# Second edge stage of a two-layer graph network: VectorE inputs from PSUM, a one-hot on ScalarE, macros of 16 groups, earlier row loads

## The chip, the cores and the metric

The kernel runs on one core of a Trainium2 chip, and the metric is the device time of that core in microseconds: the median of three runs of the whole program. A fourth execution was taken by the hardware profiler. All rows, durations and moments below are of that one.

## What is computed

Two graph layers over 6250 nodes with 128 features and 100000 edges, sorted by destination. The kernel's second edge stage, where most of the change lies, belongs to the second layer, an attention layer with four heads of 32 channels:

```python
src = jnp.concatenate([src, loop]); dst = jnp.concatenate([dst, loop])
xl = (x @ w_l + b_l).reshape(N, H, C)
xr = (x @ w_r + b_r).reshape(N, H, C)
e = jax.nn.leaky_relu(xl[src] + xr[dst], NEG_SLOPE)
logits = jnp.einsum('ehc,hc->eh', e, att)
m = jax.ops.segment_max(logits, dst, num_segments=N)
ex = jnp.exp(logits - m[dst])
denom = jax.ops.segment_sum(ex, dst, num_segments=N)
alpha = ex / denom[dst]
out = jax.ops.segment_sum(xl[src] * alpha[:, :, None], dst, num_segments=N)
```

The first layer gathers node rows by source, adds a projection of the edge features, applies relu and averages per destination. Both layers end in a residual add and a layer norm.

## The kernel before, in words

All edges lie in order of destination, 128 to a tile; four tiles (512 edges) are a group, and there are 196 groups. The destinations of one group lie within a window of 96 rows (`W`), so the sum over edges is a product with a one-hot matrix of 128 edges by 96 rows (`onehot`, L315). The window's first row comes from `first_row` (L322), which loads the group's first destination from DRAM into a register of SyncE.

The program has node stages and two edge stages. The **first edge stage** (L326 to L386) gathers one source row per edge through GpSimd (`gather`, L242, four indirect DMAs a group), adds the edge projection (L375, VectorE, PSUM input), applies relu (L377), sums with the one-hot (L380) and stores the window (L386).

The **second edge stage** (L399 to L564) goes over the groups in macros of 20 (nine of 20, then 12 and 4). For each group:

- `load_second` gathers 512 rows of `xl` (four indirect DMAs on GpSimd) and has SyncE load the window of `xr` (L424, needs `first_row`) and the destination numbers of the group, one copy in each of 96 partitions, `ds` (L426).
- `logits`: VectorE compares `ds` with the row numbers `nb` (L433) to get `at`, the transposed one-hot; TensorE transposes the four `xl` tiles into `pz` (L436) and adds `xr` times `at` (L438); ScalarE copies `pz` to `z` (L440), VectorE applies the leaky relu (L441), and TensorE multiplies by the attention weights into `plg` (L443), which collects a whole macro.
- `sums`, for the groups of the macro before: ScalarE and VectorE weight the gathered rows (`v`, L527 and L528), VectorE makes the one-hot (L315), TensorE sums (L533), VectorE scales what the group before left in its last row (`old`, L537), TensorE adds it (L539), ScalarE copies the window out of PSUM (`win`, L542), and SyncE stores it (L543, needs `first_row` again).

After a macro's last group `maxima` (L448 to L519) loads the destinations once more (`dm`, L454, four DMAs on SyncE) and works out the segment maxima and weights of all its groups in a chain of small steps over VectorE, ScalarE and TensorE. The sums of a macro can start only when its `maxima` is done, and are spread over the logits of the next one.

The order on SyncE is the order in which the code is written (`tc.manual_schedule(engines={SP})`): in each step the rows of group g+3, then the stores. On the other engines a scheduler lays out a fixed order when the program is built, by its own estimate of when each input is there; at run time each engine works through that order and stands still when the next instruction's input is late. The buffers are those named with `bufs`: 28 for the gathered rows, 5 for `xr` and `ds`, 3 for `at`, 4 for `win`, two PSUM banks each for `pz` and `pa`.

Of the kernel before, what the change touches and what calls it, by code (L numbers as in the profile page):

```python
# [8 lines left out]
F32 = mybir.dt.float32  # L9
# [6 lines left out]
P = 128  # L16
# [23 lines left out]
S = G * P  # L40
TV = -(-E // P)
NOWHERE = 1e6
MACROS = (20,) * 9 + (12, 4)
MG = max(MACROS)
HV = C + 2
CR, CC = 125, 800
# [13 lines left out]
def gnn_resnorm(  # L60
# [87 lines left out]
    def over(t, n):  # L148

        return t.unsqueeze(1).to_broadcast([t.shape[0], n, t.shape[1]])  # L150
# [96 lines left out]
    def near():  # L247
        ctx = ExitStack()
        with ctx:
# [11 lines left out]
                           allow_small_or_imprecise_dtypes=True)  # L261
            nc.gpsimd.iota(iota_p, pattern=[[0, 1]], base=0, channel_multiplier=1,
                           allow_small_or_imprecise_dtypes=True)

            with tc.tile_pool(name="ix", bufs=2) as pool, tc.tile_pool(name="ixp", bufs=2, space=PSUM) as ps:
                zero = pool.tile([P, NR // P * H * HV], F32, name="zero", bufs=1)
                nc.gpsimd.memset(zero, 0.0)
                for t, n in ((sum_t, W0), (out_t, H * HV)):
                    nc.scalar.dma_start(t.rearrange("(p r) d -> p (r d)", p=P), zero[:, 0:NR // P * n])
                nc.scalar.dma_start(xr_t[NP:NR, :], zero[:, 0:D])  # L270

                fst = pool.tile([1, GN], I32, name="fst", bufs=1)
                nc.sync.dma_start(fst, bass.AP(tensor=dst.tensor, offset=dst.offset, ap=[[S, 1], [S, GN], [1, 1]]))
                fst_f = pool.tile([1, GN], F32, name="fst_f", bufs=1)
                nc.vector.tensor_copy(fst_f, fst)
                pb = ps.tile([P, GN], F32, name="pb", bufs=1)
                nc.tensor.matmul(pb, ones[0:1, :], fst_f, start=True, stop=True)
                bb = pool.tile([P, GN], F32, name="bb", bufs=1)
                nc.vector.tensor_copy(bb, pb)
                nc.vector.tensor_scalar(nb, bb, iota_p, None, op0=OP.add)  # L280
                step = pool.tile([P, GN], F32, name="step", bufs=1)
                nc.vector.memset(step, 0.0)
                nc.vector.tensor_sub(step[:, 1:], bb[:, 1:], bb[:, 0:GN - 1])
                nc.vector.tensor_scalar(sel, step, iota_p, None, op0=OP.is_equal)


                TR = 112
                for name, ap, pad in (("src", src, 0), ("dst", dst, int(NOWHERE))):
                    rows = pool.tile([TR, T // TR, P], I32, name="rows")
                    nc.vector.memset(rows[:, T // TR - 1, :], pad)  # L290
                    full = E // P
                    o = T - TR
                    nc.sync.dma_start(rows[:, 0:T // TR - 1, :],
                                      ap[0:o * P].rearrange("(c r p) -> r c p", r=TR, p=P))
                    nc.sync.dma_start(rows[0:full - o, T // TR - 1, :],
                                      ap[o * P:full * P].rearrange("(r p) -> r p", p=P))
                    nc.sync.dma_start(rows[full - o:full - o + 1, T // TR - 1, 0:E - full * P],
                                      ap[full * P:E].rearrange("(r p) -> r p", r=1))
                    rf = pool.tile([TR, T // TR, P], F32, name="rf")
                    nc.vector.tensor_copy(rf, rows)  # L300
                    for c in range(T // TR):
                        pt = ps.tile([P, TR], F32, name="pt")
                        nc.tensor.transpose(pt, rf[:, c, :], ident[0:TR, 0:TR])
                        cs = slice(c * TR, (c + 1) * TR)
                        if name == "src":
                            nc.vector.tensor_copy(src_i[:, cs], pt)
                        else:
                            nc.vector.tensor_sub(dl[:, cs].rearrange("p (g k) -> p g k", k=G),
                                                 pt.rearrange("p (g k) -> p g k", k=G),
                                                 spread(bb[:, c * TR // G:(c + 1) * TR // G], G))  # L310

            def onehot(pool, g):

                a = pool.tile([P, G, W], F32, name="a")
                nc.vector.tensor_tensor(a, over(iota_w, G), spread(dl[:, g * G:(g + 1) * G], W), op=OP.is_equal)  # L315
                return a

            def tiles_of(g):
# [80 lines left out]
            with tc.tile_pool(name="e1", bufs=3) as pool, tc.tile_pool(name="e1m", bufs=2) as mp, \  # L399
# [14 lines left out]
                        nc.vector.tensor_copy(attw[mg][hs, (h + 1) * mg:(h + 1) * mg + 1], att_c[hs])  # L414
                XG, XR, DS = {}, {}, {}

                def load_second(g):
                    XG[g] = pool.tile([P, G, D], F32, name="xg", bufs=MG + 8)
                    if len(tiles_of(g)) < G:
                        nc.vector.memset(XG[g], 0.0)  # L420
                    for t in tiles_of(g):
                        gather(XG[g][:, t - g * G, :], xl_t, src_i, t)
                    XR[g] = pool.tile([W, D], F32, name="xr", bufs=5)
                    nc.sync.dma_start(XR[g], xr_t[bass.ds(first_row(g), W), :])  # L424
                    DS[g] = pool.tile([W, S], F32, name="ds", bufs=5)
                    nc.sync.dma_start(DS[g], bass.AP(tensor=dpad.tensor, offset=dpad.offset + 1 + g * S,  # L426
                                                     ap=[[0, W], [1, S]]))

                def logits(m, g):

                    g0, mg, plg = m
                    at = pool.tile([W, S], F32, name="at")
                    nc.vector.tensor_scalar(at, DS.pop(g), nb[0:W, g:g + 1], None, op0=OP.is_equal)  # L433
                    pz = ps.tile([P, S], F32, name="pz")
                    for j in range(G):
                        nc.tensor.matmul(pz[:, j * P:(j + 1) * P], XG[g][:, j, :], ident, is_transpose=True,  # L436
                                         start=j == 0, stop=False, skip_group_check=True)
                    nc.tensor.matmul(pz, XR.pop(g), at, start=False, stop=True, skip_group_check=True)  # L438
                    z = pool.tile([P, S], F32, name="z")
                    nc.scalar.copy(z, pz)  # L440
                    nc.vector.scalar_tensor_tensor(z, z, SLOPE, z, op0=OP.mult, op1=OP.max)  # L441
                    i = g - g0
                    nc.tensor.matmul(plg, attw[mg][:, mg - i:mg - i + H * mg], z, start=i == 0, stop=i == mg - 1)  # L443

# [78 lines left out]
                def sums(m, g, wm, cb):  # L523
                    i = g - m[0]
                    xg = XG.pop(g)
                    v = pool.tile([P, G, H, HV], F32, name="v")
                    nc.scalar.copy(v[:, :, :, 0:2], wm[:, :, :, :, i].rearrange("p j k h -> p j h k"))  # L527
                    nc.vector.tensor_tensor(v[:, :, :, 2:], xg.rearrange("p j (h c) -> p j h c", h=H),  # L528
                                            wm[:, :, 0, :, i].unsqueeze(3).to_broadcast([P, G, H, C]), op=OP.mult)
                    a = onehot(pool, g)  # L530
                    pa = ps.tile([W, H * HV], F32, name="pa")
                    for j in range(G):
                        nc.tensor.matmul(pa, a[:, j, :], v[:, j].rearrange("p h c -> p (h c)"),  # L533
                                         start=j == 0, stop=j == G - 1)
                    if before[0] is not None:
                        old = pool.tile([W, H, HV], F32, name="old")
                        nc.vector.tensor_tensor(old, before[0].rearrange("p (h c) -> p h c", h=H),  # L537
                                                spread(cb[0:W, :, i], HV), op=OP.mult)
                        nc.tensor.matmul(pa[0:1, :], sel[0:W, g:g + 1], old.rearrange("p h c -> p (h c)"),  # L539
                                         start=False, stop=True, skip_group_check=True)  # L540
                    before[0] = pool.tile([W, H * HV], F32, name="win", bufs=4)
                    nc.scalar.copy(before[0], pa)  # L542
                    nc.sync.dma_start(out_t[bass.ds(first_row(g), W), :], before[0])  # L543

                ahead = 3
                for g in range(ahead):
                    load_second(g)
                done, g0 = None, 0
                for mg in MACROS:
                    plg = ps1.tile([H * mg, S], F32, name="plg")  # L550
# [3 lines left out]
                    for i in range(mg):  # L554
                        g = g0 + i
                        if g + ahead < GN:
                            load_second(g + ahead)
                        logits(m, g)
                        for u in todo[i * n // mg:(i + 1) * n // mg]:
                            sums(done[0], u, *done[1])  # L560
# [359 lines left out]
```

## Time and profile before

| | us |
|---|---|
| median of three runs (3266.94 to 3286.33) | 3269.77 |
| the profiled execution's own time | 2644.76 |
| its span, first to last instruction | 2643.0 |
| first edge stage, first to last gather issued | 98.1 to 1085.5 |
| second edge stage, first gather issued to last store issued | 1233.5 to 2517.5 |
| busy in the span: PE / DVE / ACT / POOL | 1664.0 / 1054.5 / 490.4 / 1623.6 |
| mean granted TensorE clock | 0.807 of full |

The profiled execution is shorter than the timed runs by 625 us. PE is TensorE, PEld its weight loads, DVE VectorE, ACT ScalarE, POOL GpSimd, and SPq the queue of SyncE. SyncE's register work and DMA issues are not counted as busy time in the page, so they have to be read from its queue in order of time. A row of a group of instructions gives line, engine, operation, output and inputs, how many, then busy us and mean ns of one, then the engine's idle time before them and what ended it. In waits the three numbers are us in total, times and the longest.

### The profile page before, as it was taken

Reading aid. Unit: us, or ns where it says so; the run is one execution under the profiler, and the core shown is the slowest. Engines: PE = TensorE matmul, PEld = TensorE weight load, DVE = VectorE, ACT = ScalarE, POOL = GpSimd, SP = SyncE. Lnnn points to the kernel's source line nnn. Section 1 sums busy time; section 2 is a strip of 40 time slices with the busy share of each in tenths; the row PEclk is TensorE's granted clock in tenths of the full one; section 3 lists DMA queues with packets and bytes.
Section 4 is the critical chain, followed back from the end, with each engine's and each line's share of the span. In section 5 each row is a group of like instructions: output and inputs, shape, how many; then the busy total and the mean of one; then the engine's idle time right before and its main releaser. Section 6 shows DMA issues by size and latency. Waiting matters only on the chain.

```text
span 2643.0 us, 29233 instructions
## 1 busy us (share of the span) xinstructions
PE 1664.0 (63%) x7133; PEld 1004.1 (38%) x7133; DVE 1054.5 (40%) x2386; ACT 490.4 (19%) x1369; POOL 1623.6 (61%) x1574
## 2 busy tenths in 40 slices
PE   5376666666666666444677767776767777677500
PEld 3254444444444444322233433343434344343300
DVE  4322222222222222375233534353535445354578
ACT  1122222222222212110111212121212112121101
POOL 0477777777777777302777776767676776763000
PEclk9678887888878877766788888888888889898655
DMA  4633334333433333222323333333333333332021
GB/s 117 184 88 84 85 87 93 87 87 86 95 86 86 87 93 84 70 67 84 102 73 98 93 100 88 100 85 102 84 99 85 94 96 86 101 85 66 17 57 49
DMA packets 289799, 232.01 MB, mean 88 GB/s; under 512 B 140697, under 2 KB 244487, under 8 KB 289362
## 3 DMA queue, kind: packets, MB, share of 16 engines
q1 hardware_dynamic: 231466, 116.99, 16.5%
q0 software_dynamic: 50048, 102.60, 16.1%
q10 hardware_dynamic: 8104, 10.46, 1.1%
q8 instruction: 60, 0.98, 0.2%
q14 instruction: 121, 0.99, 0.1%
HBM read 189.85 MB, written 40.03 MB: 87 GB/s over the span
## 4 chain that ended last, share of the span: by engine, by line
POOL 28%; issue 20%; DMA 16%; PE 14%; DVE 13%; SPq 7%; ACT 2%; DVEq 0%; ACTq 0%; POOLq 0%
POOL xg L242 28%; DMA ds<-dpad 7%; SPq L322 5%; DMA xg<-xw_t,src_i 4%; PE pa L533 3%; PE pz L438 3%; PE plg L443 2%; DMA xg<-xl_t,src_i 2%; DVE z L441 2%; PE pw L231 1%; DVE v L528 1%; PE pw L205 1%; PE pa L539 1%; DVE at L433 1%; DMA xr_t<-zero 1%
## 5 line engine op out<-in xcount | busy, mean ns | idle before, releaser
L242 POOL DMA_INDIRECT xg<-xl_t,src_i x782 | 867.3, 1109 | 454.2 <-issue 212.4
L242 POOL DMA_INDIRECT xg<-xw_t,src_i x782 | 749.5, 958 | 259.1 <-issue 224.9
L373 PE MATMUL ph<-wc,fT 128*128 128x256 f32 x784 | 289.9, 501 | 283.0 <-ACT fT L370 283.0
L443 PE MATMUL plg<-z,attw 128*80 128x512 f32 (+2 forms) x392 | 260.0, 752 | 175.3 <-DVE z L441 175.0
L375 DVE TENSOR_TENSOR xg<-ph,xg 128x512 f32<-128x512 f32 x196 | 135.6, 692 | 544.0 <-DMA xg<-xw_t,src_i 433.5
L433 DVE TENSOR_SCALAR at<-ds,nb 96x512 f32<-96x512 f32 x196 | 99.3, 507 | 573.6 <-DMA ds<-dpad 519.8
L438 PE MATMUL pz<-at,xr 96*128 96x512 f32 x392 | 254.4, 737 | 86.8 <-DVE at L433 86.7
L380 PE MATMUL pa<-msg,a 128*96 128x129 f32 x1568 | 269.5, 325 | 53.9 <-ACT msg L377 53.9
L373 PEld LDWEIGHTS ph<-wc,fT 128*128 128x128 f32 x784 | 177.0, 253 | 328.7 <-ACT fT L370 303.0
L315 DVE TENSOR_TENSOR a<-iota_w,dl 128x384 f32<-128x384 f32 x392 | 216.7, 554 | 208.4 <-PE pa L380 202.0
L533 PEld LDWEIGHTS pa<-v,a 128*96 128x96 f32 x1568 | 227.4, 184 | 117.8 <-issue 98.2
L533 PE MATMUL pa<-v,a 128*96 128x136 f32 x1568 | 258.0, 310 | 8.4 <-DVE v L528 6.3
L380 PEld LDWEIGHTS pa<-msg,a 128*96 128x96 f32 x1568 | 220.4, 194 | 108.5 <-ACT msg L377 60.9
L377 ACT ACTIVATE msg<-xg 128x512 f32<-128x512 f32 x196 | 123.5, 630 | 723.0 <-DVE xg L375 723.0
L440 ACT COPY z<-pz 128x512 f32<-128x512 f32 x196 | 114.9, 586 | 731.0 <-PE pz L438 712.9
L436 PE MATMUL pz<-ident,xg 128*128 128x128 f32 x784 | 168.4, 312 | 54.2 <-DMA xg<-xl_t,src_i 48.4
L436 PEld LDWEIGHTS pz<-ident,xg 128*128 128x128 f32 x784 | 106.0, 156 | 213.8 <-issue 125.1
L441 DVE SCALAR_TENSOR_TENSOR z<-z 128x512 f32<-128x512 f32 x196 | 133.8, 684 | 58.7 <-ACT z L440 56.5
L443 PEld LDWEIGHTS plg<-z,attw 128*80 128x80 f32 (+2 forms) x392 | 56.3, 173 | 240.5 <-DVE z L441 203.4
L528 DVE TENSOR_TENSOR v<-xg,wm 128x512 f32<-128x512 f32 x196 | 132.5, 685 | 31.9 <-issue 13.6
L438 PEld LDWEIGHTS pz<-at,xr 96*128 96x128 f32 x392 | 73.6, 232 | 116.9 <-DVE at L433 114.0
L382 PE MATMUL pa<-win,sel 96*1 96x129 f32 x390 | 86.6, 310 | 12.8 <-ACT win L385 12.4
(162 smaller groups left out, 1160.3 us busy)
## 6 DMA issues: line engine op xcount, KB each, us to landing
ds<-dpad SPq DMA_DIRECT2D x196, 192.0 KB
ef<-in_edge_attr_dram SPq DMA_DIRECT2D x48, 512.0 KB
xg<-xw_t,src_i POOLq DMA_INDIRECT x782
xg<-xl_t,src_i POOLq DMA_INDIRECT x782
out_t<-win SPq DMA_DIRECT2D x196, 51.0 KB
sum_t<-win SPq DMA_DIRECT2D x196, 48.4 KB
xr<-xr_t SPq DMA_DIRECT2D x196, 48.0 KB
out_t<-zero ACTq DMA_DIRECT2D x1, 3400.0 KB
```

Source lines behind the costliest of these rows:

```text
L242: nc.gpsimd.indirect_dma_start(out=to, out_offset=None, in_=table[0:NP, :], in_offset=bass.IndirectOffsetOnAxis(ap=index[:, t:t + 1], axis=0))
L315: nc.vector.tensor_tensor(a, over(iota_w, G), spread(dl[:, g * G:(g + 1) * G], W), op=OP.is_equal)
L322: return nc.sync.value_load(dst[g * S:g * S + 1].rearrange("(p t) -> p t", p=1), min_val=0, max_val=N - 1)
L373: nc.tensor.matmul(ph[:, 2 * i:2 * i + 2, :], fT[:, i, :], wc, start=True, stop=True)
L375: nc.vector.tensor_add(xg, ph, xg)
L380: nc.tensor.matmul(pa, a[:, j, :], msg[:, j, :], start=j == 0, stop=j == G - 1)
L436: nc.tensor.matmul(pz[:, j * P:(j + 1) * P], XG[g][:, j, :], ident, is_transpose=True, start=j == 0, stop=False, skip_group_check=True)
L438: nc.tensor.matmul(pz, XR.pop(g), at, start=False, stop=True, skip_group_check=True)
L441: nc.vector.scalar_tensor_tensor(z, z, SLOPE, z, op0=OP.mult, op1=OP.max)
L443: nc.tensor.matmul(plg, attw[mg][:, mg - i:mg - i + H * mg], z, start=i == 0, stop=i == mg - 1)
L528: nc.vector.tensor_tensor(v[:, :, :, 2:], xg.rearrange("p j (h c) -> p j h c", h=H), wm[:, :, 0, :, i].unsqueeze(3).to_broadcast([P, G, H, ...
L533: nc.tensor.matmul(pa, a[:, j, :], v[:, j].rearrange("p h c -> p (h c)"), start=j == 0, stop=j == G - 1)
```

## The change

Four edits, most of them in the second edge stage. VectorE takes one input from PSUM in three places: the one-hot's row numbers (`iota_q`, a copy in a PSUM bank, in both edge stages), the second operand of the leaky relu (`pz` itself), and the window of the group before (`pa` itself, no longer its copy). The transposed one-hot moves from VectorE to ScalarE, as relu(1 − |ds − row|) in place in `ds`, with `nb` negated. Macros have 16 groups (eleven of 16, then 12, 4, 4), and the gathered rows have 30 buffers, 14 more than a macro. `load_second` is split: gathers are begun 4 groups ahead and `xr` and `ds` 7 ahead, with 9 buffers each.

```diff
-MACROS = (20,) * 9 + (12, 4)
+MACROS = (16,) * 11 + (12, 4, 4)
...
+            kps = ctx.enter_context(tc.tile_pool(name="nearp", bufs=1, space=PSUM))
+            iota_q = kps.tile([P, W], F32, name="iota_q")
+            nc.vector.tensor_copy(iota_q, iota_w)
...
-                nc.vector.tensor_scalar(nb, bb, iota_p, None, op0=OP.add)
+                nc.vector.tensor_scalar(nb, bb, iota_p, -1.0, op0=OP.add, op1=OP.mult)
...
-                nc.vector.tensor_tensor(a, over(iota_w, G), spread(dl[:, g * G:(g + 1) * G], W), op=OP.is_equal)
+                nc.vector.tensor_tensor(a, over(iota_q, G), spread(dl[:, g * G:(g + 1) * G], W), op=OP.is_equal)
...
-                def load_second(g):
-                    XG[g] = pool.tile([P, G, D], F32, name="xg", bufs=MG + 8)
+                def gather1(g):
+                    XG[g] = pool.tile([P, G, D], F32, name="xg", bufs=MG + 14)
...
-                    XR[g] = pool.tile([W, D], F32, name="xr", bufs=5)
+
+                def load_rows(g):
+                    XR[g] = pool.tile([W, D], F32, name="xr", bufs=9)
                     nc.sync.dma_start(XR[g], xr_t[bass.ds(first_row(g), W), :])
-                    DS[g] = pool.tile([W, S], F32, name="ds", bufs=5)
+                    DS[g] = pool.tile([W, S], F32, name="ds", bufs=9)
...
-                    at = pool.tile([W, S], F32, name="at")
-                    nc.vector.tensor_scalar(at, DS.pop(g), nb[0:W, g:g + 1], None, op0=OP.is_equal)
+
+                    at = DS.pop(g)
+                    nc.scalar.activation(at, at, AF.Abs, bias=nb[0:W, g:g + 1])
+                    nc.scalar.activation(at, at, AF.Relu, bias=ones[0:W, 0:1], scale=-1.0)
...
-                    nc.vector.scalar_tensor_tensor(z, z, SLOPE, z, op0=OP.mult, op1=OP.max)
+                    nc.vector.scalar_tensor_tensor(z, z, SLOPE, pz, op0=OP.mult, op1=OP.max)
...
-                    before[0] = pool.tile([W, H * HV], F32, name="win", bufs=4)
-                    nc.scalar.copy(before[0], pa)
-                    nc.sync.dma_start(out_t[bass.ds(first_row(g), W), :], before[0])
-
-                ahead = 3
+                    before[0] = pa
+                    win = pool.tile([W, H * HV], F32, name="win", bufs=4)
+                    nc.scalar.copy(win, pa)
+                    nc.sync.dma_start(out_t[bass.ds(first_row(g), W), :], win)
+
+                ahead, early = 4, 7
+                for g in range(early):
+                    load_rows(g)
                 for g in range(ahead):
-                    load_second(g)
+                    gather1(g)
...
                         if g + ahead < GN:
-                            load_second(g + ahead)
+                            gather1(g + ahead)
+                        if g + early < GN:
+                            load_rows(g + early)
                         logits(m, g)
```

## The prediction

> **What bounds the kernel now.** I read the page's chain of waits first, then the rows of the second edge stage (1233 to 2522 us), then the issues on SyncE's queue in order of time, then VectorE beside GpSimd. The page's chain names GpSimd's gathers:
>
> ```profile
> POOL xg L242 28%; DMA ds<-dpad 7%; SPq L322 5%; DMA xg<-xw_t,src_i 4%; PE pa L533 3%; PE pz L438 3%; PE plg L443 2%; DMA xg<-xl_t,src_i 2%; DVE z L441 2%; PE pw L231 1%; DVE v L528 1%; PE pw L205 1%; PE pa L539 1%; DVE at L433 1%; DMA xr_t<-zero 1%
> L242 POOL DMA_INDIRECT xg<-xl_t,src_i x782 | 867.3, 1109 | 454.2 <-issue 212.4
> L242 POOL DMA_INDIRECT xg<-xw_t,src_i x782 | 749.5, 958 | 259.1 <-issue 224.9
> L433 DVE TENSOR_SCALAR at<-ds,nb 96x512 f32<-96x512 f32 x196 | 99.3, 507 | 573.6 <-DMA ds<-dpad 519.8
> ```
>
> The same gather means 958 ns in the first stage and 1109 in the second. And VectorE spends 520 us of the second stage waiting for `ds` rows, which SyncE issues. So the next view is SyncE's issues around one macro boundary (start us, length us):
>
> ```profile
> 1701.20 0.33 SPq L543 DMA_DIRECT2D out_t<-win  x1
> 1703.62 0.34 SPq L424 DMA_DIRECT2D xr<-xr_t  x1
> 1704.00 0.43 SPq L426 DMA_DIRECT2D ds<-dpad  x1
> 1706.48 0.33 SPq L543 DMA_DIRECT2D out_t<-win  x1
> 1708.80 0.34 SPq L424 DMA_DIRECT2D xr<-xr_t  x1
> 1709.18 0.43 SPq L426 DMA_DIRECT2D ds<-dpad  x1
> 1711.69 0.33 SPq L543 DMA_DIRECT2D out_t<-win  x1
> ...
> 1729.05 1.48 SPq L454 DMA_DIRECT2D dm<-dpad  x4
> 1732.75 0.34 SPq L424 DMA_DIRECT2D xr<-xr_t  x1
> 1733.19 0.37 SPq L426 DMA_DIRECT2D ds<-dpad  x1
> 1746.89 0.33 SPq L543 DMA_DIRECT2D out_t<-win  x1
> ```
>
> Between two DMAs with a row number from `first_row` lie about 2.05 us (1704.43 to 1706.48, 1706.81 to 1708.80): the two register loads of L322. One group takes 5.2 us of SyncE with nothing idle in it. The stall is the last gap: 1733.56 to 1746.89, of which 2.05 are loads and some 11.3 are a wait for `win`. It is seen at every macro:
>
> ```profile
> SPq L543 <- ACT win L542: 120.2, 25, 14.8
> SPq L543 <- ACT v L527: 36.6, 4, 35.7
> ...
> L543 SPq DMA_DIRECT2D out_t<-win x196: 319/332/342, 1374.4 to 2517.2; - x196
> ```
>
> (SyncE's waits: us, times, longest; then the line's first and last start.) The 196 stores span 1143 us; 121 of it is waiting for `win` (36 came before the first store), so SyncE works 1022 us out of 1143, and nothing else is that full: in 1374 to 2407 us PE is busy 761 of 1033 us, GpSimd 759 (with 0.30 us of issue per gather 961), VectorE 477, ScalarE 202. From the store at 1622.46 to that at 1746.89 are 124.4 us for 20 groups: 1.5 for `dm`, 11.3 stall, 5.58 a group. **The second stage is bound by SyncE, plus a stall per macro.** The first stage is bound by GpSimd: 782 gathers of 958 ns and 0.30 us of issue are 984 us of the 987 between its first gather (98.1) and its last (1085.5).
>
> **What the Trainium skill says.** SBUF — State Buffer, "Who interferes with whom": VectorE instructions with two SBUF inputs hold off a GpSimd instruction that reads SBUF, and `tensor_scalar` in its 2-port mode holds off GpSimd altogether. The trace agrees:
>
> ```profile
> 1716.71 0.95 POOL L242 DMA_INDIRECT xg<-xl_t,src_i  x1 [0.30 <-issue]
> 1717.82 0.68 DVE L441 SCALAR_TENSOR_TENSOR z<-z 128x512 f32<-128x512 f32 x1
> 1717.96 1.82 POOL L242 DMA_INDIRECT xg<-xl_t,src_i  x1 [0.30 <-issue]
> 1718.42 0.55 DVE L315 TENSOR_TENSOR a<-iota_w,dl 128x384 f32<-128x384 f32 x1
> 1718.88 0.29 DVE L537 TENSOR_TENSOR old<-win,cb 96x136 f32<-96x136 f32 x1
> ```
>
> A gather with VectorE quiet takes 0.95 us; one that starts under a train of two-SBUF-input instructions ends when the train does. ScalarE: Activation LUTs, "Table sets": relu and abs are in every table set, so no reload; no run here shows it yet. Advanced Engine Details and Errata, "Clock Domains": a slower power profile stretches every sequencer and GpSimd cost 1.18 to 1.25 times. The profiled execution took 2644.8 us (span 2643.0), the median of the runs is 3269.8, 1.236 times as much; no row says why, and that page is the one reading I have. I sum against 2644.8 and multiply by 1.236. If instead the 625 us are a constant, the gain below is a fifth smaller.
>
> **The change, part by part.**
>
> *VectorE's inputs.* L315 takes `iota_q` from PSUM, L441 takes `pz`, L537 takes `pa`; L433 goes. Left with two SBUF inputs per group is only L528 (0.69 us). PSUM costs VectorE about nothing (L375 with a PSUM input 692 ns, L528 without 685). GpSimd's excess in the first stage is (958−940)×782 = 14 us; I take 11 back, and the stage is GpSimd's, so the end moves: **−11**. In the second the excess is (1109−940)×782 = 132 us, and I expect some 110 gone, gathers at about 0.97 us. There it lies behind SyncE (5.1 us a group against 5.6): **0**. If SyncE were not the limit it would be the largest item; see the fourth rival.
>
> *One-hot on ScalarE.* Removed: 196×0.507 = 99 us of VectorE. Added: two ACTIVATEs of 512 elements with a pointer bias. The nearest row is L510 `exp` of 80x512 at 629 ns; by the ScalarE page ("What ACT_TABLE_LOAD costs") a pointer bias makes it about 707 ns, an estimate. So 1.4 us a group: ScalarE goes from 1.2 to 2.6 us of a 5.6 us group. Hidden, **0**, so long as ScalarE does not stand at this pair waiting for `ds` while `z` and `win` copies are behind it. Bounds: −0 to +2.1 us a group (third rival).
>
> *`pz`, `pa` held longer.* `pz` is now freed by L441, not L440: some 0.8 us later, two banks, a turn of about 3.5 us for two groups against 11. `pa` waits for the next group's L537, which no longer needs the `win` copy. **0**, bounds ±5 us.
>
> *Macros of 16.* The first store cannot come before the first macro's logits and maxima are done, and in that time GpSimd is the pace: 4 groups fewer at 5.0 us: **−20**. Macros go from 11 to 14, three more sets of four `dm` loads on SyncE at 1.5 us: **+4**. The maxima's instructions keep their length of 512, and there are three more sets (about 8 us of VectorE each), beside SyncE's work.
>
> *14 spare buffers.* GpSimd's boundary waits (70.4 us on `pw` L516, 7 times) go. Not on SyncE's path: **0**; it lets gathers be there when logits run ahead.
>
> *Rows 7 ahead.* SyncE issues the same instructions per group: value loads, `xr`, `ds`, store. Its 1022 us stay. What can move is the stall. Today `z` of a macro's last group stands on VectorE behind `at` of a group two later, so the maxima start only when SyncE has issued that row (z79 at 1724.5, right after the `at` at 1724.08 that waited 4.90 us for its `ds`); the first `win` of the new macro follows 22 us later. With rows 7 ahead the logits can run up to four more groups, 22 us, in front of SyncE's stores, so the maxima can be done when SyncE arrives. But the lead must be earned: logits and sums need about 4.7 us a group (923 us of PE over 196) against SyncE's 5.6, so 16 groups win back 14 us, and behind each row that lands late ScalarE now stalls in order. I take 4 us left of 11.2 at ten inner boundaries (40), 20 at the two short macros at the end (27 now) and 4 of small waits: 64 for 121: **−57**, bounds +22 to −105.
>
> Sum: −11 −20 +4 −57 = −84. 2644.8 − 84 = 2560.8; times 1.2363 = **3166 us**, 3.2% below the median.
>
> **Rivals.**
> *A, no stall is left.* 16 us remain: −105 in place of −57, sum −132, 2512.8, times 1.2363 = 3107. For it: the lead of four groups is as long as the maxima. Against: the lead has to be rebuilt each macro.
> *B, the stalls stay.* ScalarE's pair is placed at once behind each landing row, so `z` copies are as tied to SyncE as `at` ties them now: ten inner boundaries at 11.2, the end at 27 and 4: 143, +22; sum −5, 3264. For it: the 520 us of today's `at` waits show that the order on an engine was laid out for rows earlier than they come.
> *C, slower: a loop through SyncE.* If ScalarE's queue holds the pair for the row issued after store g in front of `win` of group g+1, each group takes copy 0.27 + issue 0.33 + loads 2.05 + `xr` 0.38 + `ds` landing 2.91 (1704.00 to `at` 1706.91) + pair 1.41 + hand-overs 0.3, about 7.7 us in place of 5.6. It decides as soon as fewer than two `win` copies lie between store and pair. 173 groups still load rows after the first store: +363, and −11 −20 +4: +336, 2980.8, 3685. Against: today VectorE runs sums four groups ahead of the store (four `win` buffers), which gives the loop that many groups.
> *D, GpSimd was the pace.* If SyncE's loads shorten when GpSimd's traffic is smoother, the gathers end at 1233 + 196×5.0 = 2213 in place of 2407, with 6 groups more left for the tail (+34): −160 −11 = −171, 2473.8, 3058. For it: 28% of the chain. Against: GpSimd waits only at boundaries, SyncE nowhere else.
>
> **How the numbers follow.** Forecast 0.45, A 0.20, D 0.13, B 0.12, C 0.10. The forecast's own range is 3110 to 3235. About 1% (33 us) is what a measurement can tell from no change: faster is forecast, A and D, 0.78; within 1% is B, 0.12; slower is C, 0.10. The range reaches from D to B, 3055 to 3275, and leaves out C and what lies beyond D.
>
> **What would show it.** Right: gathers near 0.97 us in the second stage; first store near 1343 us; stores still 5.2 to 6 us apart with no idle SyncE between; SyncE's waits on `win` near 64 us; GpSimd's `pw` wait gone. Stalls of 11 us at every macro mean B; stores 7 us and more apart with ScalarE waiting for `ds` mean C; stores under 5.2 us apart mean D. The forecast is wrong at its root if SyncE shows idle time inside a macro.

## The result and the profile after

The changed kernel takes **3539.4 us** (median; 3524.9 to 3548.2), the kernel before beside it 3268.4 us. The ratio is 1.083, 95% interval 1.075 to 1.090: slower by 8%, where 3166 us had been forecast.

The changed kernel's profile has long stops, in which TensorE, VectorE and ScalarE all stand still; the profile of before (2644.8 us) has none, and there is no profile of before at its longer time. On four later visits to a chip before took 2633 to 2645 us (the change 2670 and 2658 on two of them), and on a fifth before took 3361. So the 8% have two parts, told apart below: what the change does by itself (+0.8 to +0.9%), and the rest, which goes with the stops.

Three rows of the changed kernel's page (busy, mean ns | idle before, releaser) and the first line of its chain of waits:

```profile
another core or an unknown queue 15%; PE 13%; SPq 7%; issue 7%; DVE 5%; DMA 3%; ACT 3%; POOL 1%; DVEq 0%; ACTq 0%; POOLq 0%
...
L242 POOL DMA_INDIRECT xg<-xl_t,src_i x782 | 758.0, 969 | 1046.7 <-PE pw L523 493.8
L242 POOL DMA_INDIRECT xg<-xw_t,src_i x782 | 739.8, 946 | 631.8 <-ACT msg L380 359.9
...
L439 ACT ACTIVATE ds<-ds,nb 96x512 f32<-96x512 f32 x196 | 141.2, 721 | 321.4 <-DMA ds<-dpad 319.7
```

The gathers are as short as forecast (969 ns in the second stage for 1109, 946 in the first for 958), and an ACTIVATE of the pair takes 721 ns (707 estimated). But GpSimd is no longer 28% of the chain; "unknown queue" leads. SyncE's wait at its stores and the store line itself (issue shortest/middle/longest ns, first to last start):

```profile
SPq L551 <- ACT win L550: 159.8, 16, 15.0
...
L551 SPq DMA_DIRECT2D out_t<-win x196: 2/332/1400, 1823.7 to 3397.6; - x196
```

The wait on `win` did not shrink from 120 to 64 us, it grew to 160. And a store instruction takes 2 to 1400 ns where it took 319 to 342 before: SyncE's own instructions are disturbed.

The same kernel profiled again, on a chip where before takes 2633 us, against the recorded run, by stage: first gathers, node stage and first macro, from first to last store, rest (from and to, length; busy us and instructions of PE, PEld, DVE, ACT and POOL; TensorE clock, DMA share, GB/s). The recorded run first:

```profile
100.00:1449.00 1349.00, 622.01 (x3031) 437.91 (x3032) 233.32 (x380) 215.54 (x570) 738.33 (x781) 0.71 0.27 64
1449.00:1823.00 374.00, 154.86 (x460) 76.46 (x460) 130.03 (x376) 69.94 (x155) 114.30 (x122) 0.64 0.23 65
1823.00:3397.00 1574.00, 905.60 (x3516) 450.11 (x3514) 480.68 (x1025) 433.14 (x971) 643.71 (x662) 0.74 0.23 62
3397.00:3523.00 126.00, 1.14 (x4) 1.00 (x4) 102.13 (x303) 11.32 (x30) 0.00 (x0) 0.50 0.19 54
```

and the later run:

```profile
100.00:1076.00 976.00, 628.84 (x3100) 445.49 (x3101) 238.07 (x393) 211.47 (x582) 737.92 (x782) 0.82 0.39 89
1076.00:1352.00 276.00, 152.96 (x392) 67.61 (x391) 124.76 (x368) 65.66 (x143) 97.44 (x101) 0.69 0.30 82
1352.00:2531.00 1179.00, 868.77 (x3515) 429.30 (x3513) 479.63 (x1025) 429.96 (x971) 669.33 (x682) 0.84 0.31 85
2531.00:2657.00 126.00, 1.15 (x4) 1.00 (x4) 102.16 (x303) 11.32 (x30) 0.00 (x0) 0.51 0.19 54
```

Engine by engine the busy times are nearly the same (VectorE 233 and 238, GpSimd 738 and 738, the last stage equal to the microsecond). Only TensorE, at a lower granted clock (0.74 for 0.84 between the stores), is busy longer, 906 us for 869, which is little beside the 395 us that this stage is longer. The engines mostly stand. One such stop in the recorded run's first stage:

```profile
412.38 0.69 SPq L389 DMA_DIRECT2D sum_t<-win  x1
412.54 0.63 ACT L380 ACTIVATE msg<-xg 128x512 f32<-128x512 f32 x1 [2.00 <-issue]
...
418.58 0.95 POOL L242 DMA_INDIRECT xg<-xw_t,src_i  x1 [0.30 <-issue]
419.83 0.94 POOL L242 DMA_INDIRECT xg<-xw_t,src_i  x1 [0.30 <-issue]
420.23 0.56 DVE L318 TENSOR_TENSOR a<-iota_q,dl 128x384 f32<-128x384 f32 x1 [7.77 <-remote]
...
423.03 0.37 ACT L373 COPY fT<-pt 128x256 f32<-128x256 f32 x1 [9.86 <-remote]
423.45 0.50 PEld L376 LDWEIGHTS ph<-wc,fT 128*128 128x128 f32 x2 [10.72 <-issue]
```

ScalarE, TensorE and VectorE stand for 8 to 11 us with "remote" or "issue" as releaser, that is, with nothing in the profile to wait for; GpSimd gathers on. SyncE does not stand, it steps. Its issues in a stretch of the second stage:

```profile
1647.03 0.70 SPq L429 DMA_DIRECT2D xr<-xr_t  x1
1648.43 0.71 SPq L431 DMA_DIRECT2D ds<-dpad  x1
1659.63 0.71 SPq L429 DMA_DIRECT2D xr<-xr_t  x1
1661.03 0.70 SPq L431 DMA_DIRECT2D ds<-dpad  x1
```

The starts lie 1.40, 11.20 and 1.40 us apart, all multiples of 0.70, and an issue takes 0.70 us where it took 0.34 or 0.43. SyncE's register instructions, which this view leaves out, do the same: of the 1174 plain ones (ALU_OP and SEQ_ASSERT, median 20 ns in the undisturbed traces) 107 take 0.68 to 0.715 us in this trace, and none does in the two undisturbed traces of the change. Work that an engine has begun keeps its length (in the same stretch a `z` copy takes 0.59 us, a half of ScalarE's pair 0.72). So what is slow in a stop, on SyncE at least, is the step from one instruction to the next.

### The profile page after: what moved, and what is told of

The parts are those of the page before. It is cut to its first block, busy times and chain, and to the rows that moved or that the text cites. A ratio compares the mean times of both kernels' runs of the same rounds, so it can differ in the third digit from the quotient of the medians.

```text
span 3523.1 us, 29416 instructions
## 1 busy us (share of the span) xinstructions
PE 1727.7 (49%) x7175; PEld 992.4 (28%) x7175; DVE 996.3 (28%) x2254; ACT 742.9 (21%) x1776; POOL 1504.7 (43%) x1574
## 4 chain that ended last, share of the span: by engine, by line
another core or an unknown queue 15%; PE 13%; SPq 7%; issue 7%; DVE 5%; DMA 3%; ACT 3%; POOL 1%; DVEq 0%; ACTq 0%; POOLq 0%
SPq L325 5%; PE pa L540 4%; PE plg L450 4%; DMA ds<-dpad 3%; PE pz L445 2%; PE pz L443 1%; PE pa L546 1%; POOL xg L242 1%; ACT ds L439 1%; SPq L551 1%; DVE z L448 1%; SPq L429 1%; ACT z L447 1%; SPq L431 0%
## 5 line engine op out<-in xcount | busy, mean ns | idle before, releaser
L242 POOL DMA_INDIRECT xg<-xl_t,src_i x782 | 758.0, 969 | 1046.7 <-PE pw L523 493.8
L318 DVE TENSOR_TENSOR a<-iota_q,dl 128x384 f32<-128x384 f32 x392 | 216.1, 552 | 849.5 <-remote 467.6
L450 PE MATMUL plg<-z,attw 128*64 128x512 f32 (+2 forms) x392 | 269.9, 777 | 354.5 <-DVE z L448 234.3
L448 DVE SCALAR_TENSOR_TENSOR z<-z,pz 128x512 f32<-128x512 f32 x196 | 134.1, 684 | 560.2 <-ACT z L447 393.8
L540 PE MATMUL pa<-v,a 128*96 128x136 f32 x1568 | 281.5, 334 | 8.7 <-ACT v L534 8.7
L445 PE MATMUL pz<-ds,xr 96*128 96x512 f32 x392 | 251.3, 728 | 32.9 <-ACT v L534 16.2
L546 PE MATMUL pa<-old,sel 96*1 96x136 f32 x390 | 89.2, 316 | 348.4 <-issue 215.1
L439 ACT ACTIVATE ds<-ds,nb 96x512 f32<-96x512 f32 x196 | 141.2, 721 | 321.4 <-DMA ds<-dpad 319.7
L450 PEld LDWEIGHTS plg<-z,attw 128*64 128x64 f32 (+2 forms) x392 | 43.7, 158 | 482.3 <-DVE z L448 304.5
L373 ACT COPY fT<-pt 128x256 f32<-128x256 f32 x196 | 65.9, 370 | 508.6 <-remote 402.4
```

Source lines behind the costliest of these rows:

```text
L242: nc.gpsimd.indirect_dma_start(out=to, out_offset=None, in_=table[0:NP, :], in_offset=bass.IndirectOffsetOnAxis(ap=index[:, t:t + 1], axis=0))
L318: nc.vector.tensor_tensor(a, over(iota_q, G), spread(dl[:, g * G:(g + 1) * G], W), op=OP.is_equal)
L439: nc.scalar.activation(at, at, AF.Abs, bias=nb[0:W, g:g + 1])
L448: nc.vector.scalar_tensor_tensor(z, z, SLOPE, pz, op0=OP.mult, op1=OP.max)
```

## The experiments

Ratios are to the kernel before, run beside each kernel on the same chip. A visit is one such occasion. A stall is SyncE's idle time before the first store of a macro, at the boundary between two macros; the first macro's, which has no store to follow, is not counted. The lead is how long before SyncE's last store of one macro the last `z` of the next is done.

**Before, again** (no edit).

> The kernel before, unchanged, profiled again. Theory 1 (the first profile caught an execution that lacks the common stalls of all engines; the timed runs of before have them): time near 3268 us, the span of its profile near it, first-stage gathers from about 98 to 1350-1480 us in place of 1085, with gaps of 10-15 us in which PE, VectorE, ScalarE and SyncE all stand. Theory 2 (the stalls belong to the change): the profile again shows gathers ending near 1085 us, or a first stage stretched evenly by about 1.24 to 1220 us, without such gaps.

2644.8 us (32 runs of before beside it: 2644.5); gathers of the first stage from 100 to 1087 us, SyncE's wait on `win` 124 us. The trace looks as theory 2 said, the time as neither did. Both theories fall: the profile of before was no odd execution, and the stops are not bound to the change either (below it runs without them). Within each visit all runs of before lie within 1.2% of each other, so the stops go with the visit. They do not go with the chip alone, as far as the numbers of the chips tell: on number 1 before took 2645 us on one visit and 3361 on another.

**Only `iota_q`.**

```
+kps = ...tile_pool(name="nearp", bufs=1, space=PSUM); iota_q = kps.tile([P, W], F32)
+nc.vector.tensor_copy(iota_q, iota_w)
-tensor_tensor(a, over(iota_w, G), ...)
+tensor_tensor(a, over(iota_q, G), ...)
```

> Only the iota_q copy in PSUM and its use in onehot. Theory 1 (stalls common to both kernels, not from the change): first stage as long as in the kernel before run beside it, within 1%; time within 1% of before or up to 2% faster as the gathers shorten from 1.1 to about 1.0 us. Theory 2 (iota_q sets the first stage's stalls): the first stage is some 300 us longer than before's and the whole kernel 5% or more slower.

0.994 (0.991 to 0.997): theory 1. The first stage's gathers fall from 957 to 944 ns and end 11.8 us earlier (1075.3 for 1087.1), 1.2 us of which is an earlier start; 11 had been forecast.

**Only the one-hot on ScalarE.**

```
-tensor_scalar(at, DS.pop(g), nb[...], None, op0=OP.is_equal)
+at = DS.pop(g)
+activation(at, at, AF.Abs, bias=nb[...]); activation(at, at, AF.Relu, bias=ones[...], scale=-1.0)
 ...                                              # nb negated where it is made
```

> Only the one-hot at as Abs and Relu on ScalarE, ds in place (5 buffers), nb negated. Theory 1 (the loss of the change is ScalarE's pair waiting in order for ds, with win and z copies behind it): 4 to 8% slower, stores of the second stage 7 us and more apart, SyncE idle inside macros. Theory 2 (ScalarE has room): within 2% of before, stores as far apart as before.

1.002 (1.000 to 1.003): theory 2. The second stage's gathers fall from 1146 to 1016 ns, by more than with `iota_q` alone (1077), and the last store does not come earlier (2521.9 us for 2520.2): the end was not GpSimd's.

**Only the macros.**

```
-MACROS = (20,) * 9 + (12, 4);    xg bufs=MG + 8
+MACROS = (16,) * 11 + (12, 4, 4); xg bufs=MG + 14
```

> Only macros of 16 groups and 14 spare row buffers. Theory 1 (each boundary costs a fixed stall, and three more boundaries cost three more of 11 to 30 us): 1 to 3% slower. Theory 2 (the shorter prologue pays for them): within 1% of before.

1.012 (1.010 to 1.014): theory 1. The first store comes 20.4 us earlier (1355.9 for 1376.3), as forecast; but there are 13 stalls of 10 to 15 us for 10, and SyncE's wait on `win` rises from 124 to 156 us.

**The whole change, again.**

> The whole change, again. In the last call the kernel before took 2644 us on its chip, not 3268, and showed no stalls of all engines. Theory 1 (the 8% belong to executions with stalls of all engines, where the change meets more of them): beside a kernel before of 2644 us the change takes between 2560 us (the sum of the prediction) and 2700 us, a ratio under 1.02. Theory 2 (the change is slower by itself, through its macros and the order of its ScalarE work): ratio 1.06 to 1.10, about 2860 us, at any pace of the kernel before.

1.008 (1.005 to 1.011), 2670 us: theory 1. SyncE's wait on `win` is 162 us.

**Only rows and gathers earlier.**

```
-ahead = 3: load_second(g + 3)             (xr, ds bufs=5)
+ahead, early = 4, 6: gather1(g + 4), load_rows(g + 6)   (xr, ds bufs=8)
```

> Only the gathers 4 groups ahead in place of 3, and the rows xr and ds begun 6 groups ahead (8 buffers each; 9 with the at tiles of before don't fit). Theory 1 (the stall at a boundary is the ds row that is issued late; earlier rows end it): SyncE's waits on win shrink from 120 us to under 70, 2 to 4% faster. Theory 2 (the stall is the length of maxima itself, and no lead is built): stalls of 11 us stay, within 1% of before.

1.015 (1.012 to 1.017): theory 2 as to the stall, which stays (125 us of waits), and neither as to the time. A lead is built, though (16 us for 3.5), so theory 2's reason fails. The 40 us come from SyncE: its second register load before a store takes 700 ns on average for 477, at each of the 170 groups whose store follows a row load. Why is open; the whole change, with rows 7 ahead, does not show it (485).

**The change with macros of 20 and 8 spare buffers.**

> The whole change, but with macros of 20 groups and 8 spare row buffers as before. Theory 1 (the macros of 16 carry a loss of about 1%, as alone): 20 to 40 us faster than the whole change run beside it. Theory 2 (short macros and spare buffers are needed by the rest of the change): slower than the whole change by 1% or more.

0.996 (0.995 to 0.997), 35 us faster than the whole change: theory 1. The waits on `win` are 128 us, so the rest of the change does not shrink the stall there.

**The change with rows and gathers 3 ahead.**

> The whole change, but with gathers and rows begun 3 groups ahead, together, as before (5 buffers each). Theory 1 (rows 7 ahead bring what gain there is): slower than the whole change by 2% or more. Theory 2 (rows ahead bring nothing): within 1% of the whole change.

1.017 (1.014 to 1.020), 0.9% slower than the whole change: theory 2 by its number, but not "nothing". A stall is 15.3 us at most boundaries here against 12.3 in the whole change, and the lead is 2 us, so beginning rows and gathers earlier does bring 3 us each (the two were not tested apart).

Why not all? In every trace of the whole change the logits do run ahead: the lead is 18 to 20 us at nine of the ten inner boundaries (3.5 us in the kernel before). A boundary of the undisturbed run above, on SyncE, then on ScalarE and VectorE:

```profile
1638.77 0.33 SPq L551 DMA_DIRECT2D out_t<-win  x1
1639.21 1.77 SPq L461 DMA_DIRECT2D dm<-dpad  x4
1642.87 0.34 SPq L429 DMA_DIRECT2D xr<-xr_t  x1
1643.25 0.42 SPq L431 DMA_DIRECT2D ds<-dpad  x1
1658.82 0.33 SPq L551 DMA_DIRECT2D out_t<-win  x1
```

```profile
1623.76 0.56 ACT L465 COPY lg<-plg 64x512 f32<-64x512 f32 x1
...
1642.87 0.69 DVE L468 TENSOR_TENSOR pen<-dm 64x513 f32<-64x513 f32 x1
```

`lg` is ready at 1624.3. The maxima start at 1642.9, 18.6 us later, when `dm` has landed; and `dm` stands in SyncE's written-out order behind the last store. From there to the next store are 16 us. The lead is gained and thrown away. So the next edit moves `dm`, whose contents depend on nothing but `dpad`:

**`dm` at the macro's start**, in the whole change, in the kernel before, and in the change with macros of 20.

```
 plg = ps1.tile(...); m = (g0, mg, plg)
+load_dm(g0, mg)          # the four dma_start of L461, taken out of maxima
 for i in range(mg): ...
```

> The whole change, with the four dm loads of a macro issued by SyncE at the macro's start in place of after its last store and rows. In the changed kernel the logits of a macro end 18 to 20 us ahead of SyncE's last store, yet the maxima start 4 us after it, when dm has landed. Theory 1 (the lead is there and dm's place in SyncE's order throws it away): the stalls of 12 us at 13 boundaries shrink to under 4, the time falls by 100 to 150 us against the whole change, to 2520-2570 us where before takes 2645. Theory 2 (maxima are late because their instructions queue behind sums that wait for stores): the stalls stay at 11-12 us, time within 1% of the whole change's 2670.

> The kernel before, with the four dm loads of a macro issued at its start. Before has a lead of only 3.5 us between a macro's last logits and SyncE's last store. Theory 1 (without rows ahead only the landing of dm is saved): stalls fall from 12 to about 8 us, 20 to 40 us faster, ratio 0.985 to 0.993. Theory 2 (dm's place was the whole stall even before): stalls under 4 us, 80 to 110 us faster. Theory 3 (dm is no link of the chain): within 0.5% of before.

> The whole change but with macros of 20 and 8 spare row buffers as before, and the dm loads at the macro's start. Theory 1 (the 14 spare buffers are what lets the logits run ahead; with 8 the lead was 2 to 8 us): stalls fall only to 6-10 us, 2590-2620 us, slower than the whole change with early dm. Theory 2 (fewer boundaries count for more than the lead): faster than that version, about 2520 us.

The change: 0.988 (0.986 to 0.989), about 2% less than without. Before: 0.978 (0.977 to 0.980). The change with macros of 20: 0.972 (0.970 to 0.973). `dm` was a link, for the kernel before as well: 56 us, where its theory 1 gave 20 to 40; its eight inner stalls are 8 us, as that theory had them, and the two of the short macros at the end are gone. The third kernel keeps 8.5 us on average at its inner boundaries and is the fastest of the three, so both its theories have a part. For the change itself neither theory holds: the stalls at the end shrink to 4 us and less, but the ten inner ones only fall from 12.3 to 10.7 us, and the lead is gone: the last `z` now ends 2 us before the last store. The rows are there, and ScalarE's queue shows why they don't help:

```profile
1811.78 0.72 ACT L439 ACTIVATE ds<-ds,nb 96x512 f32<-96x512 f32 x1 [3.38 <-DMA ds<-dpad]
1812.53 0.72 ACT L440 ACTIVATE ds<-ds,ones 96x512 f32<-96x512 f32 x1
1813.16 0.56 ACT L447 COPY z<-pz 128x512 f32<-128x512 f32 x1
...
1816.83 0.72 ACT L439 ACTIVATE ds<-ds,nb 96x512 f32<-96x512 f32 x1 [2.00 <-DMA ds<-dpad]
```

The `z` copy of 1813.16 stands behind a pair that waits for the row just issued, which belongs to a group several later: counted over groups 20 to 169, 4.7 `z` copies of earlier groups are still to come when a pair runs, 31 us before its own. By the Trainium skill (PSUM — Partial Sum Buffer, "Engine vs sequencer instructions") ScalarE's queue is strictly first in, first out; the trace agrees: in most groups ScalarE waits 1 to 4 us for a row, 2.9 on average, and the `z` copy comes only after the pair.

**The pair held to two groups ahead**, on top of the change with `dm` early.

```
-at = DS.pop(g)                                   # in place, 9 buffers
+ds, at = DS.pop(g), pool.tile([W, S], F32, name="at", bufs=2)
 (xg bufs=MG + 11)
```

> The whole change with dm early, and the pair's result in its own at tile with 2 buffers (11 spare row buffers so that it fits), so that ScalarE can't do a pair more than two groups ahead of its logits. Theory 1 (the pairs for rows far ahead, waited for in order, tie z to SyncE): the lead between a macro's last z and SyncE's last store grows from 2 to 10 us or more, stalls fall from 10.5 to under 4 us, 60 to 110 us faster than the change with dm early alone (2605 us). Theory 2 (the pairs are not what ties): stalls and time within 1% of it.

0.970 (0.968 to 0.971), 2553 us. Exactly one `z` copy is now behind a pair, the lead is 24 us, and the stalls fall from 10.7 to 6 us: theory 1 in direction, but its numbers are missed (stalls under 4 us, 60 to 110 us faster; it is about 50). What is left follows `dm` once more, that of the macro after. On VectorE, then on SyncE:

```profile
1600.51 0.74 DVE L510 SCALAR_TENSOR_TENSOR mx<-fp,prev,sm 64x512 f32<-64x512 f32 x1
1618.62 0.69 DVE L474 TENSOR_TENSOR pen<-dm 64x513 f32<-64x513 f32 x1 [17.37 <-DMA dm<-dpad]
1619.23 0.20 DVE L513 SCALAR_TENSOR_TENSOR sc<-pen,prev,mx 64x1 f32<-64x1 f32 x1
```

```profile
1614.78 0.33 SPq L557 DMA_DIRECT2D out_t<-win  x1
1615.22 1.75 SPq L461 DMA_DIRECT2D dm<-dpad  x4
...
1627.98 0.33 SPq L557 DMA_DIRECT2D out_t<-win  x1
```

The maxima use the lead as far as `mx`. Then the next macro's `pen` stands on VectorE ahead of the rest of them (`sc` and what follows) and waits 17.4 us for a `dm` that SyncE issues behind the last store. Over the run these waits are 172 us, at 11 boundaries.

**Four sums left over.**

```
+late += [(done, u) for u in ...]        # sums of the macro before
+n = max(0, len(late) - 4); todo, late = late[:n], late[n:]
 ...                                     # the four are emitted after maxima
```

> The whole change with dm early, and the last four groups' sums (and stores) of every macro left over until after the next macro's maxima, so that SyncE has four stores to issue while maxima are worked out. Theory 1 (the stall is the length of maxima, some 15-20 us, with nothing for SyncE to do): stalls under 2 us at the inner boundaries, about 100 us faster than with dm early alone, 2490-2520 us. Theory 2 (sums also wait in order behind the maxima's instructions on VectorE and ScalarE): stalls of 5 us or more stay, under 50 us faster. Theory 3 (then GpSimd's gathers set the pace): no stalls, but stores 5.3 us and more apart with SyncE idle between.

**0.947 (0.945 to 0.948), 2494 us**: theory 1, with all its numbers. The store row of this kernel and SyncE at a boundary:

```profile
L556 SPq DMA_DIRECT2D out_t<-win x196: 319/332/346, 1344.4 to 2367.2; - x196
```

```profile
1594.16 0.33 SPq L556 DMA_DIRECT2D out_t<-win  x1
1594.60 1.75 SPq L460 DMA_DIRECT2D dm<-dpad  x4
...
1601.09 0.33 SPq L556 DMA_DIRECT2D out_t<-win  x1
...
1607.65 0.33 SPq L556 DMA_DIRECT2D out_t<-win  x1
```

The 196 stores span 1023 us (1179 in the whole change) with 7 us of waiting; here the maxima run from about 1596 to 1610 while SyncE goes on storing. This although ScalarE's pairs stand far ahead again (5.6 `z` copies). The edit also puts the next macro's `dm` ahead of the four stores, and `pen` never waits for it here (172 us before); whether moving that `dm` alone would have ended the stalls was not tested.

**Whether it comes back on another chip** (no edit).

> The kernel before on one more chip, for a profile beside that of the change. Theory 1 (most chips run it without stalls of all engines): 2645 us, first-stage gathers from 98 to 1085 us. Theory 2 (this chip stalls all engines as the recorded comparison's did): about 3268 us, first-stage gathers to 1400 us or more, and the share of the extra time by stage can be read from this profile.

> The whole change on one more chip. If before takes about 2645 us here, theory 1 (the change itself costs three more boundary stalls, less the shorter first stage): ratio 1.005 to 1.012. If before takes about 3268 us here, theory 2 (stalls of all engines cost the change more): ratio 1.06 to 1.10; theory 3 (the 8.3% was a difference between two visits to a chip): ratio 1.00 to 1.03.

2643 us, and 1.009 (1.008 to 1.011): theory 1 again.

**What is left of the change**: three versions with `dm` early and four sums left over, on a visit where before took 3361 us.

> As the version with dm early and four sums left over (2494 us), but with macros of 20 groups and 10 spare row buffers. Theory 1 (with no stall at the boundaries, their number counts for nothing but the shorter prologue of 16): 10 to 25 us slower than it. Theory 2 (the maxima's own work on PE and VectorE still costs): 5 to 30 us faster.

> The kernel before with PSUM inputs for VectorE, dm early and four sums left over: one-hot on VectorE, macros of 20, 8 spare row buffers, gathers and rows 3 groups ahead. Theory 1 (moving the one-hot and beginning rows early bring little; the stall was all): within 1% of the version with macros of 20, the same additions and the rest of the change. Theory 2 (rows only 3 ahead leave ds late with the stall gone): 40 us or more slower than it, with VectorE waiting for ds.

> The version with dm early and four sums left over (2494 us), with each group's row number loaded once by SyncE and kept in a register for the store, so that a group costs SyncE about 3.2 us in place of 5.2. Theory 1 (SyncE's loads bound it, GpSimd's gathers at 1.27 us each are next at 5.07 us a group): stores 5.1 us apart, 20 to 40 us faster. Theory 2 (SyncE was only keeping pace with another bound): within 10 us. Theory 3 (other SyncE traffic, such as loads from DRAM, slowed the gathers): over 60 us faster.

Macros of 20: 0.949 (0.944 to 0.954); the version with macros of 16 (0.947) ran on another visit, so neither theory can be told. One-hot on VectorE, rows 3 ahead, macros of 20: 0.952 (0.947 to 0.957); theory 1, so ScalarE's one-hot and the early rows are worth nothing that can be told once the stall is gone. One row load, macros of 16: 0.940 (0.934 to 0.945), about 1% under the first; SyncE then waits 178 us on `win`,

```profile
SPq L557 <- ACT win L556: 178.4, 91, 10.3
```

which it does for 3 us in the version with macros of 20, so it is no longer the bound. Theory 1 is favoured, but with stops in the trace and another macro size beside it the 20 to 40 us aren't measured cleanly.

These three traces have the stops too. As intervals over 3 us in which TensorE, VectorE and ScalarE all do nothing, the first stage has 57 of them (429 us) in the recorded run, 59 to 63 (503 to 518 us) in these three, 34 (142 us) in the undisturbed run of the whole change; the first stage is 1349 us long in the recorded run, about 1380 in the three and 976 undisturbed. In the second stage (first gather to 70 us before the end) the recorded run has 63 (512 us, against 35 undisturbed), the version with macros of 20 has 19 (168 us, most of it before its first store), and it goes from first to last store in 1198 us against 1574. In the recorded run most of the long ones come about three to a macro, 10 to 50 us behind its first store; the two versions with macros of 20 have next to none there after their first macros, the one with one row load has some of 3 to 7 us. No run tells why.

## Why the prediction was wrong, point by point

*The step that failed: what goes of the stall.* "64 for 121: −57". It became 162, +41, outside the bounds given for it, and in the undisturbed pair this alone turns a gain of 2.7% (25.6 − 98 us) into a loss of 1%. The lead was earned as argued (19 us for 3.5), but the sum took `dm` as 1.5 us of SyncE's issue and never as a wait: `pen` can't start before it lands, and it is issued after the last store. Asking who waits for that issue would have found it: in the lines that the prediction shows, `dm` at 1729.05 stands between the last store and the stall, and in the same trace VectorE has

```profile
1732.33 0.69 DVE L461 TENSOR_TENSOR pen<-dm 80x513 f32<-80x513 f32 x1 [0.63 <-DMA dm<-dpad]
```

So the maxima of before, too, waited for `dm` at last, not for the row of a group two later, as the prediction read it. Three more boundaries then cost three more stalls of 12 us, not +4; the sum also counted one of them too few at the end (two short macros, where 12, 4 and 4 make three stalls, 38 us in the trace). Rival B had the effect (stalls of 11 us at every macro) and, with `dm` out of the way, its mechanism: ScalarE's pair at once behind each landing row.

*The other step that failed: "times 1.2363".* The sum was made against a profile without stops and stretched evenly for runs with them, on the reading of the Trainium skill (Advanced Engine Details and Errata, "Clock Domains") that a slower power profile stretches each sequencer and GpSimd cost. The traces do not agree: no such cost was stretched (gathers 946 and 944 ns in the first stage, the last 126 us equal). The time is in stops, which depend on the stage and the version. Had the undisturbed 2670 been known, times 1.2363 it gives 3301, +1%; the other 238 us to 3539 are more than an even stretch, or the constant that the prediction named beside it (3295), would give. That the change loses more to the stops than before does is what the medians say; where before has its own was never seen, as no trace of before was taken on such a visit.

*In the sum's own terms*, the undisturbed pair (spans 2646.1 and 2671.6): first stage −11 forecast, −10.9 to the second stage's first gather; prologue of a macro −20, here −12.8 (−19.0 with the macros alone); SyncE's work between stores +4, +6.7; its idle time before stores −57, +41.0; other idle time +1.6. −84 forecast, +25.6 measured.

*Right:* gathers at 0.97 us and worth nothing to the end; the second stage bound by SyncE's register loads, about 5.2 us a group within the macros of every undisturbed trace (5.3 with rows 6 ahead); ScalarE's one-hot at no cost by itself, with 4 table loads before and after, though its place in the queue held the lead back once `dm` was early, as the prediction's condition for its 0 had feared; GpSimd's extra as VectorE's doing, of which taking the one-hot's `tensor_scalar` off VectorE removed more (130 ns a gather) than `iota_q` did (69 ns), beside a before of 1146 ns whose other traces have 1109 and 1119. *Rival C* fell: with stores 5.2 us apart between boundaries there is no loop. *Rival D* fell: the gathers got shorter and SyncE's loads didn't.

*What stays open:* what stops the engines on some visits, why the change loses more to it than before, and the slow register loads with rows 6 ahead. The stops were seen with GpSimd gathering on, SyncE stepping in multiples of 0.70 us and no transfer of the profile to wait for; nothing here was able to switch them on or off. Whether recording the trace has a part in them was not tested.

## What to carry to other kernels

When a queue's order is written out by hand, a stage's lead is worth only what the last issue in that order allows: list for each stall every transfer that its first instruction needs, small ones above all, and where it is issued, and the transfers of the next block whose users are placed among that block's instructions. Here the stall went when the issuing queue was left some work of the block before. And where a profile and the timed runs disagree by 24%, don't bridge them with a factor, which failed here: take the profile of a run with the time that is to be explained.

## What the runs showed that was not expected

TensorE, VectorE and ScalarE can stand together for 5 to 18 us, dozens of times in a run, without any wait in the profile, while GpSimd gathers on: 2633 to 2645 us on some visits is 3268 to 3361 us on others for the same kernel. SyncE's plain instructions show it first: a store issue of 319 to 342 ns became 2 to 1400, and its instructions start multiples of 0.70 us apart. And `dm`, a transfer of four small issues a macro, held the maxima up twice: its own macro's, and then, as the next macro's, the one before.
